# A four-layer graph kernel: attention sums that begin inside the decay layer, and zero counts moved into the first loop

## The chip, the cores and the metric

The kernel runs on one core of a Trainium2 chip. The metric is the device time of one execution in microseconds. A core has a matrix engine (PE, with its weight loads shown as PEld), a vector engine (DVE), a scalar engine (ACT), a general engine (POOL) and a queue engine (SP) that here issues nearly all DMAs. Each takes its instructions in order; semaphores tie them together.

## The reference

3327 nodes with 64 features `x` and a 0/1 matrix `adj` (3327 x 3327) go through four layers of the form `x = x + layer(relu(layernorm(x)))`:

- Layers 0 and 3 are hyperbolic attention: for each pair of nodes a sigmoid weight times `adj`, times a function (an arctangent) of the pair's inner products, then a weighted sum over neighbours.
- Layer 1 (the decay) weights a node's neighbours by their rank: `rank = cumsum(mask, axis=1)`, `w = mask * DECAY ** (k - pos)`, `out = w @ (h @ W) + bias`, with at most 100 neighbours.
- Layer 2 (the attention with gates) needs `(A > 0) @ h` with the diagonal of `adj` left out, an average of neighbours, and two GRU cells; their outputs are scaled by the diagonal of `adj` and added to `x`.

The kernel uses that `adj` holds only zeros and ones. It proves that on the fly: it counts the zeros and the ones of every block and compares the sum of the counts at the end; if they don't add up, a general path runs.

## The kernel before

The matrix is padded to 3328 = 26 blocks of 128 (`T` = 26), transposed, and read from memory block row by block row.

**First loop (layer 0, `hyperbolic_series`, lines 334 to 706).** Four chunks of columns (4, 3, 3 and 3 tiles of each half: 1024 or 768 columns) times 26 row blocks `b` make 104 tiles `k`. For each tile SP loads `adj` into one of four buffers (L386), ACT makes a sigmoid (L595), POOL multiplies it by `adj` (L597), PE makes the inner products (L608, L609), ACT takes the arctangent (L614), DVE combines both (L618), and PE sums over neighbours (L627, L635). An iteration `j` handles two tiles; the sigmoid and POOL's multiply are queued three tiles ahead, the load five. The order on ACT, DVE, PE and POOL is the one written in the program. Each iteration ends with `ahead.step(j)` (L1314): one DVE instruction for the next layer, alternately a mask (L1324) and a zero count (L1333) over half of a 128 x 1664 piece ("quarter") of `adj`, for the first twelve (`EARLY`) row blocks of layer 1, from four buffers of their own.

**Decay (layer 1, `plain_decay`, lines 1358 to 1604).** Two column halves `c` times 26 blocks make 52 steps `k`, in which `b` runs from 25 down to 0. `make_mask` turns a quarter of `adj` into an 8-bit mask, on POOL (L1413) or on DVE (L1410); `check` counts its zeros on DVE and issues the load that takes its buffer (L1399), of which there are seven. PE multiplies the mask by a triangular matrix to count ranks (`counts`, L1422), ACT turns counts into powers of two (`weights`, L1428), PE sums (`sums`, L1436). Twelve steps of counts run before `h` is normed; from then on each step catches up two sums until level, then does one. At the end of a half, `degrees` (L1443) copies the numbers of neighbours, `out_of` (L1451) the sums; `from_pairs` (L1256) multiplies by the layer's matrix and adds to `x`. Zero counts of the twelve quarters in `LATE` are left for layer 2.

**Attention and gates (layer 2, `plain_gat`, lines 1606 to 1803).** `norm_relu` norms all of `x`; then 26 blocks of 16 matmuls (L1708) multiply masks by two half-precision parts of `h`. Between blocks a table (`todo`) places other work: `turn` (transposes of `h`), `degrees`, `inverse`, and `check` for the `LATE` quarters, loaded a second time (L1630). Then eight GRU steps `u` (L1777): PE products (L1741, L1746), sigmoids, DVE before the tanh (L1759, L1760), tanh, and `state` on DVE (L1770 to L1774). The result is transposed back and added to `x` (L1266, L1801, L1802), outside the hand-ordered region, so that the scheduler slips it between the last states.

**Second loop (layer 3)** is the first loop's code with the 8-bit masks in place of `adj`.

Of the kernel before, what the change touches and what calls it, by code (L numbers as in the profile page):

```python
# [10 lines left out]
F32 = mybir.dt.float32  # L11
# [37 lines left out]
def tile_gnn4(ctx: ExitStack, tc: tile.TileContext, x, adjT, att0, b0, w1, bias1, w_gat, a_gat,  # L49
# [285 lines left out]
    def hyperbolic_series(r, params, ok, masks=None, done=None, ahead=None, then=None):  # L335
# [18 lines left out]
        with ExitStack() as st:  # L354
            pers = st.enter_context(room(name="hs", bufs=1))
# [235 lines left out]
            def sigmoid(k):  # L591
# [4 lines left out]
                adj = adjs.pop(k) if masks is None else halves(masks[b // 2][:, b % 2, :], c)  # L596
                G.tensor_tensor(sig, adj, sig, op=OP.mult)  # L597

# [207 lines left out]
            if then is not None:  # L806
                then(SimpleNamespace(Xr=Xr, M=M, slots=slots, later=later, factors=factors, close=lp.close,
                                     ahead=ahead))
                return
# [463 lines left out]
    LATE = *range(EARLY, EARLY + 4), *range(EARLY + 7, 2 * T - 4, 4)  # L1273
# [11 lines left out]
    class Ahead:  # L1285


        def __init__(self, masks, zo):
            self.masks, self.zo = masks, zo

        def begin(self, pool):
            self.adjs = [pool.tile([P, 2, CW], F32, name=f"ahead{k}") for k in range(4)]
# [20 lines left out]

        def step(self, j):  # L1314
# [3 lines left out]
            n = j - 2  # L1318
            q, i = divmod(n, 4)
            if 0 <= q < EARLY:  # L1320
                o, what = i // 2, i % 2
                adj = self.adjs[q % 4][:, o, :]
                if what == 0:
                    V.tensor_scalar(mask_of(self.masks, q)[:, o, :], adj, 1.0, 0.0, op0=OP.is_equal, op1=OP.add,  # L1324
                                    accum_out=self.ones, saturate=False)
                else:
                    k = q if o == 0 else 2 * T + 2 + q
                    zeros(self.same[:, o, :], adj, self.zo[:, k:k + 1])
            if n >= 3 and (n - 3) % 2 == 0 and (n - 3) // 4 < EARLY:
                self.load((n - 3) // 4 + 4, (n - 3) // 2 % 2)  # L1330
# [27 lines left out]
    def plain_decay(e, right, masks, zo, wt, bias, gru, ball_of_r):  # L1358
# [15 lines left out]
        with ExitStack() as st:  # L1374
# [12 lines left out]
            for k in (1, 0, 4, 3, 2):  # L1387
                w2 = masks[k].bitcast(BF)
                free += [w2[:, q, :].rearrange("p (o h i) -> p o h i", o=2, h=2) for q in range(2)]
            own = [pers.tile([P, 2, 2, BK], BF, name=f"w{i}") for i in range(3)]  # L1390
# [3 lines left out]
            def adj_of(k):  # L1394
                return bufs[(k - EARLY) % len(bufs)]
# [507 lines left out]
```

## Time and profile before

| | us |
|---|---|
| median of three runs (749.37 to 753.2) | 752.94 |
| the profiled execution | 750.64 |
| its span, first to last instruction | 748.8 |
| first loop, first to last sums | 34.3 to 242 |
| decay, first counts to last sums | 245.2 to 389.1 |
| attention's blocks | 408.7 to 450.4 |
| `x` of layer 2 ready | 486.6 |
| second loop, from its first sums | 516.9 to 720 |

| engine | busy us | share of the span |
|---|---|---|
| PE | 634.7 | 85% |
| ACT | 543.1 | 73% |
| DVE | 518.6 | 69% |
| POOL | 467.3 | 62% |

A profile line gives start and length, or busy time and count; `out<-in` names the tiles, and what follows a `<-` in brackets is what ended the engine's wait. "Issue" is time in which an engine waited for nothing that the profile shows. Ends of matmuls are modelled.

### The profile page before, as it was taken

The page shows a single profiled execution, that of the slowest core. Times are in us where ns is not written, and L with a number is a line of the kernel's source. Part 1 is how long each engine was busy: PE and PEld are TensorE (multiplying, and loading weights), DVE is VectorE, ACT ScalarE, POOL GpSimd, SP SyncE. Part 2 cuts the span into 40 slices and gives each one's busy share as a digit, 9 for nine tenths or more (in the row PEclk, how much of TensorE's full clock was granted, in tenths as well). Part 3 has the DMA queues.
Part 4 walks back from the last instruction along what each step waited for, and adds up shares of the span by engine and source line. Part 5 has one row for each costly group of instructions (what it writes and reads, how often), then busy time and mean ns, then how long its engine had stood idle before and what let it go on. Part 6 is the DMA issues. An engine that isn't in the chain of part 4 may idle for free.

```text
span 748.8 us, 11837 instructions
## 1 busy us (share of the span) xinstructions
PE 634.7 (85%) x4227; PEld 257.6 (34%) x4227; DVE 518.6 (69%) x909; ACT 543.1 (73%) x697; POOL 467.3 (62%) x353
## 2 busy tenths in 40 slices
PE   0799999999999788889982999328999999999950
PEld 0522233333333333434441663124223333333310
DVE  6867777777777698978828577996555555555556
ACT  2788888888887864577782369257888889889841
POOL 2699989989999002399910000036888788887830
PEclk9999999999999999999995999659999999999995
DMA  3988898988888600599813640001001001000001
GB/s 62 347 261 284 267 279 252 287 273 275 259 261 266 260 1 10 200 401 380 334 36 149 223 143 1 0 0 39 1 1 39 1 2 38 0 1 1 1 2 49
DMA packets 57028, 106.46 MB, mean 142 GB/s; under 512 B 8928, under 2 KB 33152, under 8 KB 56960
## 3 DMA queue, kind: packets, MB, share of 16 engines
q1 hardware_dynamic: 52608, 105.59, 42.5%
q10 hardware_dynamic: 4352, 0.02, 0.3%
q8 instruction: 35, 0.57, 0.3%
q14 instruction: 33, 0.27, 0.1%
HBM read 102.87 MB, written 0.88 MB: 139 GB/s over the span
## 4 chain that ended last, share of the span: by engine, by line
PE 59%; DVE 18%; ACT 8%; issue 7%; POOL 5%; DMA 1%; ACTq 1%; POOLq 0%; DVEq 0%
PE slot L627 16%; PE slot L635 9%; PE slot L608 8%; PE slot L1422 7%; PE slot L609 7%; PE bank L1708 5%; POOL sig L597 5%; PE slot L1436 4%; ACT sig L595 2%; DVE X L1473 2%; DMA adj<-in 1%; DVE mask L1410 1%; ACT slot L614 1%; ACTq L307 1%; ACT w L1428 1%
## 5 line engine op out<-in xcount | busy, mean ns | idle before, releaser
L618 DVE SCALAR_TENSOR_TENSOR sig<-slot,sig 128x768 f32<-128x768 f32 (+1 forms) x208 | 212.7, 1022 | 145.7 <-POOL sig L597 141.7
L614 ACT ACTIVATE slot<-slot 128x768 f32<-128x768 f32 (+1 forms) x208 | 177.3, 852 | 54.4 <-PE slot L609 54.2
L597 POOL TENSOR_TENSOR sig<-adj,sig 128x768 f32<-128x768 f32 (+1 forms) x104 | 201.0, 1962 | 14.2 <-ACT sig L595 10.0
L595 ACT ACTIVATE sig<-leftB,right 128x768 f32<-128x768 f32 (+1 forms) x208 | 203.2, 977 | 0.1
L597 POOL TENSOR_TENSOR sig<-mask,sig 128x768 f32<-128x768 fp8e4 (+1 forms) x104 | 173.2, 1677 | 40.4 <-ACT sig L595 35.0
L627 PE MATMUL slot<-sig,Xr 128*64 128x384 f32 (+1 forms) x832 | 169.6, 526 | 6.3 <-DVE sig L618 6.1
L608 PE MATMUL slot<-XC,XT 128*128 128x384 f16 (+1 forms) x416 | 142.2, 342 | 3.2 <-ACT sum L645 1.7
L609 PE MATMUL slot<-XF,XE 73*128 73x384 f16 (+1 forms) x416 | 141.4, 340 | 0.0
L635 PE MATMUL slot<-sig,X 128*32 128x384 f32 (+1 forms) x832 | 94.2, 525 | 0.0
L1428 ACT ACTIVATE w<-slot,ebias 128x832 bf16<-128x832 f32 x76 | 68.6, 951 | 30.7 <-PE slot L1422 30.6
L627 PEld LDWEIGHTS slot<-sig,Xr 128*64 128x64 f32 x832 | 49.6, 135 | 88.0 <-issue 61.5
L608 PEld LDWEIGHTS <-XT 128*128 128x128 f16 x416 | 40.6, 98 | 93.8 <-issue 67.4
L1422 PE MATMUL slot<-mask,rest 128*128 128x416 fp8e4 x208 | 55.0, 347 | 8.3 <-ACT mask L1428 4.2
L1413 POOL CAST mask<-ahead 128x1664 fp8e4<-128x1664 f32 x17 | 27.8, 1642 | 49.5 <-PE slot L1436 45.1
L1422 PE MATMUL slot<-mask,after 128*128 128x416 fp8e4 x208 | 54.7, 346 | 4.4 <-ACT deg L1443 2.9
L418 POOL MEMSET X<- 128x832 f32 x2 | 1.6, 791 | 84.4 <-ACT xh L1732 84.4
L1333 DVE TENSOR_SCALAR_CACHE_REDUCE same<-ahead 128x832 bf16<-128x832 f32 (+1 forms) x39 | 52.4, 1345 | 0.3
L609 PEld LDWEIGHTS <-XE 73*128 73x128 f16 x416 | 40.8, 98 | 29.7 <-issue 5.6
L1333 DVE TENSOR_SCALAR_CACHE_REDUCE same<-adj 128x1664 bf16<-128x1664 f32 x25 | 47.1, 1882 | 0.6
L1708 PE MATMUL bank<-mask,h 128*64 128x416 fp8e4 x416 | 40.1, 353 | 0.0
L635 PEld LDWEIGHTS slot<-sig,X 128*32 128x32 f32 x832 | 16.4, 108 | 67.7 <-issue 66.1
L1428 ACT ACTIVATE mask<-slot,ebias 128x832 bf16<-128x832 f32 x28 | 26.1, 952 | 11.5 <-PE slot L1422 11.3
(315 smaller groups left out, 636.6 us busy)
## 6 DMA issues: line engine op xcount, KB each, us to landing
adj<-in SPq DMA_DIRECT2D x78, 384.0 KB, 4.5
adj<-in SPq DMA_DIRECT2D x28, 832.0 KB, 6.8
ahead<-in SPq DMA_DIRECT2D x20, 832.0 KB, 8.3
adj<-in SPq DMA_DIRECT2D x27, 512.0 KB, 4.9
ahead<-in SPq DMA_DIRECT2D x32, 416.0 KB, 5.2
leftB<-left SPq DMA_DIRECT2D x6, 384.0 KB, 3.4
XC<-XT SPq DMA_DIRECT2D x12, 96.0 KB, 5.5
X<-in SPq DMA_DIRECT2D x2, 416.0 KB
```

The costliest lines, as they stand in the source:

```text
L595: A.activation(sig, leftB[c], AF.Sigmoid, bias=right[:, b:b + 1])
L597: G.tensor_tensor(sig, adj, sig, op=OP.mult)
L608: PE.matmul(L[:, o, :c[1] * P], XT[:, rows], XC[c][:, o, :], start=True, stop=False)
L609: PE.matmul(L[:, o, :c[1] * P], XE[:KE, rows], XF[c][:, o, :], start=False, stop=True)
L614: A.activation(L, L, AF.Arctan, scale=PA / SX ** 2)
L618: V.scalar_tensor_tensor(sig, slot[:, :, :tiles[k][0][1] * P], PC, sig, op0=OP.add, op1=OP.mult)
L627: PE.matmul(acc[c][o * D:(o + 1) * D, 0, :n], Xr[:, b, :], sigs[k][:, o, :], start=b == 0, stop=b == T - 1)
L635: PE.matmul(acc[c][q:q + 32, 1, :n], X0[:, b - 1 + i, :], w[:, o, :], start=b == 1, stop=b == T - 1, tile_position=(0, q))
L1333: V.tensor_scalar(same, adj, 0.0, 0.0, op0=OP.is_equal, op1=OP.add, accum_out=count)
L1422: PE.matmul(cnt[o][:, h, :BK], w, cols(k, o, h), start=w is after and steps[k][1] == T - 1, stop=True, skip_group_check=True)
L1428: A.activation(ws[k][:, o, :, :], cnt[o][:, :, :BK], AF.Exp, scale=-LN2, bias=ebias)
L1708: PE.matmul(acc[k][o * D:(o + 1) * D, :], w, mask[:, o * HP + k * BK:o * HP + (k + 1) * BK], start=b == T - 1 and i == 0, stop=b == 0 and ...
```

## The change

1. Six row blocks (`CHECKED`: b = 2, 6, 10, 11, 12, 13) have their zeros counted in the first loop, from the tile that the loop has loaded anyway: 24 counts, put on a list when the tile's POOL multiply is queued and run on DVE in the same iteration's `step`. The 48 masks and counts for the next layer are no longer one an iteration: a credit of 1.5 an iteration pays for both kinds. Their loads go out one iteration after the count.
2. `LATE` is gone, with the twelve loads and counts of layer 2. In the decay, steps of a `CHECKED` block have their mask made on DVE and no count. They are now 38 to 41, 45 and 49 in the second half, where they had been 27, 31, ... 47.
3. Catch-up steps no longer begin with two sums: one stands behind the first exponential, one behind the second. The first step of the second half and the end have an order of their own. All `degrees` but the first go to DVE.
4. Two of the four buffers of layer 1 become a pool of their own (`own`). From step 28 they take no more loads; `normed_h` writes the normed `h` of 12 of the 26 blocks there, one instruction (or pair) a step from step 33 on. Inverse roots are by `Ln` and `Exp`, whose table set is loaded at step 24.
5. `plain_gat` is called from within `plain_decay`, with its PSUM banks, inside the hand-ordered region. Blocks 0, 1 and 2 stand between the last products of the decay; then the other 14 blocks are normed (`finish`), while blocks of the first norm go on. The table `todo` and the order of blocks change; a weight product moves from ahead of the blocks to behind block 21.
6. The diagonals on POOL are made at every second step from 25 to 49 rather than at each step from 25 to 37.
7. The last transposes and updates of `x` move into the GRU loop (`last`), in program order.

```diff
@@ first loop
-                adj = adjs.pop(k) if masks is None else halves(masks[b // 2][:, b % 2, :], c)
+                adj = adjs[k] if masks is None else halves(masks[b // 2][:, b % 2, :], c)
                 G.tensor_tensor(sig, adj, sig, op=OP.mult)
+                if masks is None:
+                    ahead.see(k, b, adjs.pop(k))
...
-    LATE = *range(EARLY, EARLY + 4), *range(EARLY + 7, 2 * T - 4, 4)
+    CHECKED = 2, 6, 10, 11, 12, 13
...
+        def see(self, k, b, adj):
+            if b in CHECKED:
+                c = k // T
+                n = c * T + T - 1 - b if c < 2 else 2 * T + 2 + EARLY + (c - 2) * len(CHECKED) + CHECKED.index(b)
+                self.seen.append(lambda: zeros(self.same[:, :, :adj.shape[-1]], adj, self.zo[:, n:n + 1]))
...
+            for q, o in self.old:
+                self.load(q, o)
+            self.old, self.loads = self.loads, []
+            if j >= 2:
+                self.credit += 1.5
+                while self.seen:
+                    self.seen.pop(0)()
+                    self.credit -= 1
+                while self.credit >= 1:
+                    next(self.ops, None)
+                    self.credit -= 1
+            else:
+                while self.seen:
+                    self.seen.pop(0)()
@@ decay
-                if k not in LATE:
-                    zeros(same, adj_of(k), zo[:, k:k + 1])
-                load(k + len(bufs))
+                if steps[k][1] not in CHECKED:
+                    zeros(same, adjs[k], zo[:, k:k + 1])
+                buf = adjs.pop(k)
+                if k < T or not any(buf is t for t in ah_.own):
+                    load(next(coming), buf)
...
+                if c == 0 and o == 0:
+                    A.activation(to, cnt[o][q, :, :BK], AF.Copy, accum_out=total)
+                else:
+                    V.tensor_scalar(to, cnt[o][q, :, :BK], 1.0, 0.0, op0=OP.mult, op1=OP.add, accum_out=total)
...
+            norm0 = normed_h(slice(0, T // 4), M[:, :12, :], Xr[:, :12, :])
...
+                if k == T:
+                    counts(k - 1, 1, rest)
+                    degrees(0, 1)
+                    sum_next()
+                    for o in range(2):
+                        counts(k, o, after)
+                        weights(k, o)
+                    out_of(0)
                 elif k == K_:
                     counts(k - 1, 1, rest)
-                    degrees(steps[k - 1][0], 1)
+                    degrees(1, 1)
+                    sum_next()
+                    out_of(1)
+                else:
+                    counts(k, 0, after)
+                    weights(k, 0)
+                    if done < k - 1:
+                        sum_next()
+                    counts(k - 1, 1, rest)
+                    counts(k, 1, after)
+                    weights(k, 1)
+                    sum_next()
...
+                if k == T - 2:
+                    A.preload_act_table_set("natural_log_exp_and_others")
+                if k > T + 6:
+                    next(norm0, None)
...
+            then(H, hparts, banks, last_x, finish, close)
@@ attention
+            block(0)
+            last_x(0)
+            block(1)
+            last_x(1)
+            block(2)
+            finish()
+            close()
...
-                norm_relu(tp, hn, H.rearrange("p k o d -> p o k d"), order=(1, 0),
-                          then=lambda o: split2(*[p[:, :, o, :] for p in parts], H[:, :, o, :]))
...
+                todo = {5: lambda: turn(0), 10: lambda: degrees(0, 1), 12: lambda: degrees(2, 3),
+                        13: inverse, 15: lambda: turn(4), 17: lambda: turn(8), 19: lambda: turn(12),
+                        21: weights2}
+                for n in range(3, T):
+                    block(n)
+                    if n in todo:
+                        todo[n]()
...
+                def last(i):
+                    from_pairs(None, oP, use, None, range(4 * i, min(4 * i + 4, C2)),
+                               banks[4 + i].rearrange("p (t h d) -> p t h d", h=2, d=D))
...
+                    for i in {C + 2: (0,), C + 3: (1,), C + 4: (2, 3)}.get(u, ()):
+                        last(i)
```

The new `normed_h` norms the blocks `ks` of both halves in steps (each `yield` ends one):

```python
V.reduce_sum(s, x, axis=AX.X)
...
V.tensor_sub(mid, x, wide4(s))
...
A.activation(squares, mid, AF.Square)
...
V.reduce_sum(v, squares, axis=AX.X)
...
A.activation(y, v, AF.Ln)
A.activation(y, y, AF.Exp, scale=-0.5)
...
for o in range(2):
    V.scalar_tensor_tensor(to[:, o], mid[:, o], 0.0, y[:, o, :, None].to_broadcast([P, n, D]),
                           op0=OP.max, op1=OP.mult)
    A.activation(hi[:, o], to[:, o], AF.Copy, scale=SH)
...
for o in range(2):
    V.scalar_tensor_tensor(lo[:, o], to[:, o], SH, hi[:, o], op0=OP.mult, op1=OP.subtract)
```

## The prediction

> **What bounds the kernel now.** I read the page first, then busy time by stage, the groups, the timeline inside the first loop, and the chain of waits around the stage borders.
>
> ```profile
> span 748.8 us, 11837 instructions
> ...
> DVE  6867777777777698978828577996555555555556
> ```
>
> Two pair loops (slices 2 to 13 and 28 to 39) fill most of the span; between them stand the decay and the attention. DVE is at 70% through the first loop, 50% through the second. By stage (PE, PEld, DVE, ACT, POOL busy; granted clock; DMA share):
>
> ```profile
> 93.00:140.00 47.00, 46.33 (x304) 17.31 (x300) 36.11 (x54) 40.88 (x54) 43.96 (x25) 1.00 0.87 270
> ...
> 388.00:409.00 21.00, 5.17 (x31) 3.09 (x31) 12.97 (x21) 8.48 (x15) 0.00 (x0) 0.61 0.45 163
> 409.00:452.00 43.00, 42.92 (x442) 26.37 (x440) 29.85 (x34) 20.84 (x33) 0.00 (x0) 0.95 0.50 160
> ```
>
> The first loop is held by PE (46.3 of 47.0 us), with POOL at 94% and DMA at 87%: three resources nearly full, DVE at 77%. From 388 to 409 us PE works 5.2 of 21.0 us. This hole is what the change aims at. Then the attention's blocks are pure PE. The chain of waits shows the hole's end, and that its first four blocks (64 matmuls) run at 2.0 us each, against 2.81 us for two later:
>
> ```profile
> 394.65 1.96 DVE ln_s L144 x2
> ...
> 407.80 0.90 PE bank L1648 x2
> 408.70 8.02 PE bank L1708 x64
> ```
>
> In the first loop every weight product on DVE (L618) starts within 0.06 us of the end of POOL's multiply (L597), or directly behind a count. The timeline round tile 54 (chunk 2, b = 2), by SP, DVE and POOL:
>
> ```profile
> 138.38 2.33 SPq L386 DMA_DIRECT2D adj<-in  x2
> ...
> 142.83 1.01 DVE L1333 TENSOR_SCALAR_CACHE_REDUCE same<-ahead 128x832 bf16<-128x832 f32 x1
> ...
> 143.76 0.95 DVE L618 SCALAR_TENSOR_TENSOR sig<-slot,sig 128x768 f32<-128x768 f32 x1
> ...
> 145.87 1.82 POOL L597 TENSOR_TENSOR sig<-adj,sig 128x768 f32<-128x768 f32 x1 [0.35 <-DMA adj<-in]
> ```
>
> Tile 54's load is the second of the first line (issued about 140.2, when POOL has finished tile 50, whose buffer it takes); it lands at 145.8, just as POOL wants it. The ahead count of this iteration runs at 142.83. A count of tile 54 would stand there too, and wait 3 us.
>
> **What the skill says.** (1) The Trainium skill, "TensorE: Matmul & The Clock Gate", section "What's actually happening": PE runs at half clock after an idle window of about 3.4 us and at full clock once busy as long. The trace agrees: 0.61 in the hole, the slow first blocks after it. (2) "Perfetto Trace Analysis", section "Tensor Engine Instruction": ACT, DVE and GPSIMD are strict FIFO. So a DVE count that waits for a load holds the next L618; in the trace L618 at 143.76 stands behind the count of 142.83. (3) "DMA: Bandwidth & Descriptors", section "Anatomy of one DMA": 2.0 us plus bytes/436e9, told of another path; an estimate of 2.9 us for 384 KB. The trace has 4.5 us (median of the x78), and I use that. (4) "GPSIMD Engine Reference", section "1. Specifications": POOL shares its SBUF interface with VectorE and loses to two-port modes or two SBUF inputs. The counts read one tensor and take 0.94 us start to start for 832 elements, so no such mode; L597 keeps 1.807 us minimum, 1.826 median. I add nothing for POOL.
>
> **The change part by part.**
>
> *Zero counts in the first loop.* 24 counts are added: 6 of 1024 elements and 18 of 768. From 0.94 us for 832 (and 0.88 for an L618 of 768) I take 1.14 and 0.88: 22.7 us of DVE. DVE idles 52 us between 35 and 233 us (146.1 busy of 198), so the work itself fits; its place costs. (a) Iterations now hold 1 or 2 counts or masks, 1.5 on average, where they held 1. In steady state (tiles 43 to 47) L618 of an odd tile starts at 127.33; then 0.88 + 2 x 0.94 puts the next L618 at 130.09, its end at 131.05, while PE wants the slot for its product at 130.84: 0.2 to 0.3 us late. Every other such iteration passes it on, about 12 x 0.26 = 3 us; I take 2, since some merge with (b). (b) A count is issued at the end of the iteration in which POOL's multiply was queued, behind the iteration's second L618. For an even tile that is 2.9 to 3.0 us before POOL's start, for an odd one 0.9. Loads land 1 to 3 us ahead of POOL in this trace. Lined up tile by tile (load issue when POOL ends tile m-4, plus 4.6 us, or 6.2 in the first chunk), waits are: chunk 0, b 6, 10, 12: 2.9, 2.7, 3.1; chunk 1, b 2, 6, 10, 12: 1.3, 1.9, 0.3, 0.8; chunk 2: 2.1 to 3.0, 2.1, 0.3, 1.3; chunk 3: 1.8, 1.7, 0.6, 1.1; odd tiles about 0. The next L618 has 0.8 us to spare. Waits beyond 0.8 sum to 13 us; the 0.94 us of work that a count displaces, and POOL's own 3 us lag at the loop's start, take part back: I take 7. Sum: **+9** (from +3, all but (a) hidden, to +16, nothing taken back). The next load into a counted tile's buffer also waits for the count, but that ends before POOL's multiply does. With this count gone the stall would move nowhere else: POOL follows ACT, ACT follows PE.
>
> *Catch-up sums split.* A catch-up step takes 3.6 us (304.39, 308.11, 311.71) with ACT's exponentials exposed; split, PE alone needs about 3.0. But POOL's mask of step 24 waits for its load until 315.17, that of 25 runs 318.29 to 319.86, and PE starts step 25 at 320.03. These loads are released by DVE's checks from 305.25 on, which don't change: gain 0 to 0.2. I take **0**.
>
> *Half border.* Both degree copies stand on ACT between exponentials:
>
> ```profile
> 322.56 0.86 ACT L1443 ACTIVATE deg<-slot 64x832 f32<-64x832 f32 x1
> ...
> 325.17 0.86 ACT L1443 ACTIVATE deg<-slot 64x832 f32<-64x832 f32 x1
> ```
>
> With the second on DVE (behind a check, free at about 323.3) and the sums between, the next step's `rest` counts come at about 328.0 rather than 329.9: **-1.9** (0 to -3).
>
> *Norm of 12 blocks inside the second half.* DVE: 3 x 0.95, 4 x 0.54 and five small ones, 5.9 us over 14 steps of 2.34; DVE works 29.0 of 43.0 us there. ACT gets one 0.85 square, two 0.5 copies, two small; it idles 0.54 a step. Hidden. The table load (1.28 us in the trace) comes at step 24, where PE waits for masks anyway. Two of seven adjacency buffers retire: five loads in rotation at 2.34 us a step is 11.7 us a cycle against about 6.8 to 8.3 to land and 1.9 to check: fits, but less cover. If not, rival 3.
>
> *The hole.* The old span from the sums' end (389.1) to the blocks' end (450.4) is 61.3 us. New, back to back at full clock: wait for the last degrees on DVE 0.6; 26 blocks x 1.40 (22 warm ones took 30.9) = 36.4; the X products that move between blocks 1.17 + 0.85; turns and diagonals 2.7; weights (0.9 + 0.2) and waits for ACT copies 2.0: 43.7. The second norm (14 blocks, about 9.2 us of DVE and ACT from last X) hides behind blocks 2 to 11 (14 us). **-17.6** (-15 to -19). The 12 late checks (1.93 us each) and their loads vanish; DVE was not the bound there: 0.
>
> *Last rows inside the GRU loop.* Now in program order, each `last` sits ahead of the next PE products:
>
> ```profile
> 472.94 0.52 PE L1266 MATMUL pt<-ident,H 128*128 128x128 f32 x3 [1.16 <-ACT gate L1753]
> 476.29 0.90 PE L1266 MATMUL pt<-ident,H 128*128 128x128 f32 x3 [2.83 <-DVE H L1774]
> ```
>
> Products of step 7 (2.55 us) wait for state 5 (476.2) and one transpose; the tanh input comes at 479.2 instead of 476.15, 1.2 us of it covered by the row updates. Then 0.6 and 0.9 us for transposes at `last(1)` and `last(2)`: **+2.7** (0 to +4.5).
>
> Sum: 9 + 0 - 1.9 + 0 - 17.6 + 2.7 = **-7.8 us**. The profiled execution took 750.6 us with a span of 748.8; it becomes 741.0 and 742.8. The runs' median, 752.94, is 2.3 above that execution: **745**.
>
> **Rivals.** (1) *DVE's slack takes the counts in*: POOL and DMA run further ahead than I allow; loop +3, sum -14, **739**. For it: 52 us of DVE idle. Against: the load of tile 54 landed only as POOL began. (2) *Slower*: the counts' waits reach PE whole. The place is the DVE queue behind the second L618; the price is 24 us (the waits listed, undiminished), sum +7, **760**. It decides from a loop cost of 16.8 us. For it: PE, POOL and DMA are all near full, nothing can be made up. Against: 0.8 us of spare at each L618. (3) *The gap moves into the second half*: five buffers and DVE steps that wait for ACT starve the masks; 0.4 us a step over 20 steps, +8, **753**. Against: masks stand 6 us (step 30) to 9.6 us (step 51) ahead of PE.
>
> **Chances.** Forecast 0.50, rival 1 0.20, rival 2 0.16, rival 3 0.14. About 0.5% (3.8 us) is what tells apart from no change. Of the forecast (own range 740 to 750) a tenth lies within it. Faster 0.63, same 0.18, slower 0.19. Range 737 to 757: it leaves out the far end of rival 2 and little of rival 1.
>
> **What would show it.** The blocks begin within 1.5 us of the decay's last sums, clock 1.0 throughout; the first loop ends about 9 us later, with new DVE waits on `adj` loads, longest near b 2 and 6; steps 33 to 46 keep 2.34 us; PE stands idle ahead of the eighth GRU products. Wrong, if the loop grows by under 4 or over 15 us, or the second half's steps lengthen.

## The result and the profile after

The changed kernel takes 773.78 us (median of four runs, 771.01 to 777.49) against 752.89 for the kernel before: a ratio of 1.0292, with a 95% interval from 1.0239 to 1.0345. It is slower by 21 us, where 745 was forecast. The profiled execution took 773.8 us, 23.2 more than that of before.

The page after, span, DVE's and the DMA's rows of the 40 slices:

```profile
span 772.1 us, 11825 instructions
...
DVE  6768879778788678887684316797555555555555
...
DMA  3877887978978910297960000001001001000001
```

The late loads of layer 2 are gone: the DMA row is empty behind the decay. DVE's idle slices (4, 3, 1, at 405 to 463 us) now stand among the attention's blocks, where the kernel before had the late counts. By stage, with the same columns as before (PE, PEld, DVE, ACT, POOL busy; granted clock; DMA share; GB/s): part of the first loop, the decay's last steps, and the stretch from the last sums to the blocks' end:

```profile
100.70:152.30 51.60, 49.56 (x320) 18.51 (x320) 43.20 (x68) 43.12 (x57) 46.48 (x27) 1.00 0.85 258
399.00:414.90 15.90, 15.90 (x108) 7.04 (x108) 10.41 (x13) 10.79 (x12) 8.79 (x14) 0.99 0.16 56
414.90:465.70 50.80, 45.18 (x456) 28.65 (x454) 15.97 (x26) 20.74 (x36) 0.00 (x0) 0.97 0.01 1
```

The hole before the attention is filled: PE works 45.2 of 50.8 us at a granted clock of 0.97. The chain of waits at the place where the hole was (start, length, what):

```profile
413.73 0.41 DVE deg L1477
...
414.79 1.05 DVE deg L1477 x2
...
415.88 1.25 PE slot L1738 x12
```

Blocks begin directly behind the decay's last sums, with one wait for the last degrees. So the change does what it says, and it still loses. Stage by stage, in the two profiled executions (the blocks of the kernel before end at 450.9 us; 450.4, given above, is too early by half a microsecond):

| stage | before | after | difference | predicted |
|---|---|---|---|---|
| start to the end of the first weight product | 34.2 | 40.2 | +6.0 | 0 |
| first loop, to the last weight product | 207.9 | 219.2 | +11.3 | +9 |
| decay, first counts to last sums | 143.9 | 152.4 | +8.5 | -1.9 |
| last sums to the blocks' end | 61.7 | 50.8 | -10.9 | -17.6 |
| blocks' end to the first mean of layer 3 | 35.8 | 42.6 | +6.8 | +2.7 |
| second loop | 206.0 | 206.0 | 0 | 0 |

The differences sum to +21.7. The rest of the spans' 23.3 lies behind the last engine instruction, where no stage changed.

**The start.** DVE's timeline in the prologue after:

```profile
20.29 1.02 DVE L467 SCALAR_TENSOR_TENSOR Xp<-Xr,Xp 128x832 f16<-128x832 f32 x1
25.19 1.22 DVE L1360 TENSOR_SCALAR_CACHE_REDUCE same<-adj 128x1024 bf16<-128x1024 f32 x1 [3.88 <-DMA adj<-in]
...
26.34 1.02 DVE L467 SCALAR_TENSOR_TENSOR Xp<-Xr,Xp 128x832 f16<-128x832 f32 x1
```

The first of the new counts (tile 2) stands between the two halves of one prologue step, and waits 3.9 us for its load. It was written behind the prologue, in iteration -1, but needs nothing except its load, and the scheduler orders the prologue: the count was carried up. The first weight product comes 6 us late.

**The first loop.** The groups of the page (count, busy and mean ns, then idle time before and what ended most of it) show who waits now:

```profile
L598 POOL TENSOR_TENSOR sig<-adj,sig 128x768 f32<-128x768 f32 (+1 forms) x104 | 201.8, 1962 | 31.5 <-ACT sig L596 27.4
...
L611 PE MATMUL slot<-XC,XT 128*128 128x384 f16 (+1 forms) x416 | 142.5, 342 | 11.6 <-DVE sig L621 9.6
...
L1360 DVE TENSOR_SCALAR_CACHE_REDUCE same<-adj 128x768 bf16<-128x768 f32 (+2 forms) x40 | 54.5, 1362 | 18.0 <-DMA adj<-in 17.6
```

DVE's counts wait 17.6 us for `adj` loads: 3.9 us is tile 2's wait in the prologue, 2.0 us falls in the decay, and 11.7 us in the loop (from the list of waits between 35 and 260 us: total, how often, longest):

```profile
DVE same L1360 <- DMA adj<-in: 11.7, 9, 3.1
```

PE waits 9.6 us for DVE's weight products. One such place on DVE, and on POOL the multiplies around it:

```profile
155.47 0.95 DVE L1360 TENSOR_SCALAR_CACHE_REDUCE same<-adj 128x768 bf16<-128x768 f32 x1 [3.12 <-DMA adj<-in]
...
156.34 1.01 DVE L1327 TENSOR_SCALAR_CACHE_REDUCE mask<-own 128x832 fp8e4<-128x832 f32 x1
...
157.28 1.82 DVE L621 SCALAR_TENSOR_TENSOR sig<-slot,sig 128x768 f32<-128x768 f32 x2
```
```profile
153.50 1.82 POOL L598 TENSOR_TENSOR sig<-adj,sig 128x768 f32<-128x768 f32 x1 [0.24 <-DMA adj<-in]
155.51 1.81 POOL L598 TENSOR_TENSOR sig<-adj,sig 128x768 f32<-128x768 f32 x1 [0.20 <-DMA adj<-in]
```

The count and POOL's multiply at 155.51 wait for the same load. The weight product of the tile that POOL finished at 155.32 stands behind that count and a mask: it starts at 157.28, 2 us late. This is the strict order of DVE's queue that the prediction drew from the Trainium skill ("Perfetto Trace Analysis", section "Tensor Engine Instruction"), and the trace agrees.

**The decay.** Most steps of the second half take 2.34 us as before, but 43, 44 and 45 take 5.50, 5.04 and 4.03: 14.6 instead of 7.0. DVE, SP and POOL there:

```profile
387.03 1.03 DVE L1437 TENSOR_SCALAR mask<-adj 128x1664 fp8e4<-128x1664 f32 x1 [4.09 <-DMA adj<-in]
387.97 1.88 DVE L1360 TENSOR_SCALAR_CACHE_REDUCE same<-ahead 128x1664 bf16<-128x1664 f32 x1
```
```profile
377.13 6.11 SPq L1425 DMA_DIRECT2D adj<-in  x3
389.93 2.81 SPq L1425 DMA_DIRECT2D ahead<-in  x2
```
```profile
380.77 1.57 POOL L1440 CAST mask<-adj 128x1664 fp8e4<-128x1664 f32 x1 [10.68 <-DMA adj<-in]
...
388.74 1.57 POOL L1440 CAST mask<-ahead 128x1664 fp8e4<-128x1664 f32 x1
```

Two things meet. POOL has waited 10.7 us for the load of step 42's mask and is late from there: its mask of step 44 (388.74) ends when PE already waits for it. And DVE's mask of step 45 waits 4.1 us for its load; the count behind it, which would release a buffer, waits with it, so that SP issues no load between 383.2 and 389.9. DVE's steps of the norm stand in that queue too, and pass the delay on to ACT. The waits from 383 to 402 us:

```profile
ACT own L1585 <- POOL mask L1440: 6.4, 1, 6.4
...
PE slot L1451 <- POOL mask L1440: 3.0, 1, 3.0
PE slot L1451 <- ACT w L1457: 2.6, 1, 2.6
```

PE's first wait makes step 43 long. The second makes step 44 long: ACT's exponential stands behind a copy of the normed `h` (L1585), which starts at 393.63, when DVE has written its input (the first of two L1583 ends at 393.55; POOL's mask, which the list names, was done by 393.1). Step 45 is long because PE then runs at a granted clock of 0.58.

**Blocks and tail.** Between the blocks PE waits for DVE's use of a diagonal, and longest for a copy on ACT:

```profile
434.95 0.37 PE L1785 MATMUL slot<-diag,ones_bf 128*64 128x416 bf16 x2 [0.68 <-DVE deg L1792]
...
450.60 1.11 PE L1774 MATMUL slot<-ident,own 128*128 128x128 f32 x4 [3.51 <-ACT xh L1779]
451.64 4.09 PE L1738 MATMUL slot<-mask,own 128*64 128x416 fp8e4 x32
```

The two blocks behind that wait take 4.09 us where two others take 3.00. In the kernel before, four matmuls of two diagonals ran without a wait between them:

```profile
420.07 0.52 PE L1669 MATMUL bank<-diag,ones_bf 128*64 128x416 bf16 x4
```

And in the tail the eighth GRU products stand behind a transpose that waits for a state:

```profile
489.07 0.87 PE L1269 MATMUL slot<-ident,own 128*128 128x128 f32 x3 [3.58 <-DVE own L1875]
...
492.43 0.47 PE L1269 MATMUL slot<-ident,own 128*128 128x128 f32 x1 [2.48 <-DVE own L1875]
...
492.83 3.04 PE L1842 MATMUL slot<-xh,gw 128*64 128x416 f32 x8
```

The products themselves then take 3.04 us where seven others took 1.62 to 2.15. The granted clock is 0.50 from 488.0 to 497.6 us: PE comes back from idling at half clock, as the Trainium skill's "TensorE: Matmul & The Clock Gate", section "What's actually happening", says.

### The profile page after: what moved, and what is told of

It is laid out like the page before. It is cut to its first block, busy times and chain, and to the rows that moved or that the text cites. A ratio compares the mean times of both kernels' runs of the same rounds, so it can differ in the third digit from the quotient of the medians.

```text
span 772.1 us, 11825 instructions
## 1 busy us (share of the span) xinstructions
PE 646.0 (84%) x4227; PEld 259.5 (34%) x4227; DVE 522.3 (68%) x946; ACT 538.1 (70%) x693; POOL 465.0 (60%) x353
## 4 chain that ended last, share of the span: by engine, by line
PE 39%; DVE 16%; issue 15%; POOL 13%; DMA 7%; ACT 7%; ACTq 1%; POOLq 0%; SPq 0%; DVEq 0%
PE slot L630 11%; POOL sig L598 8%; PE slot L638 6%; DMA adj<-in 6%; PE slot L611 6%; PE slot L612 5%; PE slot L1738 3%; POOL mask L1440 3%; PE slot L1451 3%; ACT sig L596 2%; DVE X L1506 1%; PE slot L1842 1%; PE slot L1465 1%; DVE same L1360 1%; DVE sig L621 1%
## 5 line engine op out<-in xcount | busy, mean ns | idle before, releaser
L598 POOL TENSOR_TENSOR sig<-adj,sig 128x768 f32<-128x768 f32 (+1 forms) x104 | 201.8, 1962 | 31.5 <-ACT sig L596 27.4
L1360 DVE TENSOR_SCALAR_CACHE_REDUCE same<-adj 128x768 bf16<-128x768 f32 (+2 forms) x40 | 54.5, 1362 | 18.0 <-DMA adj<-in 17.6
L1738 PE MATMUL slot<-mask,own 128*64 128x416 fp8e4 x416 | 39.8, 346 | 0.4 <-DVE deg L1477 0.4
L1440 POOL CAST mask<-ahead 128x1664 fp8e4<-128x1664 f32 x8 | 12.6, 1570 | 44.0 <-PE slot L1465 44.0
L1457 ACT ACTIVATE mask<-slot,ebias 128x832 bf16<-128x832 f32 x28 | 25.7, 951 | 16.3 <-PE slot L1451 15.6
L1465 PE MATMUL slot<-w,h 128*64 128x416 bf16 x304 | 36.1, 362 | 0.0
```

The source lines that it names most:

```text
L1360: V.tensor_scalar(same, adj, 0.0, 0.0, op0=OP.is_equal, op1=OP.add, accum_out=count)
L1457: A.activation(ws[k][:, o, :, :], cnt[o][:, :, :BK], AF.Exp, scale=-LN2, bias=ebias)
L1738: PE.matmul(acc[k][o * D:(o + 1) * D, :], w, mask[:, o * HP + k * BK:o * HP + (k + 1) * BK], start=n == 0 and i == 0, stop=n == T - 1 and ...
```

## The experiments

Each run changes the changed kernel unless it says otherwise. Times are medians, ratios are to the kernel before on the same chip. The changed kernel's own ratio is 1.0292, so a ratio of 1.0219 means 0.73 points, some 5.5 us, won back. By these ratios no repair tried alone is clear of the changed kernel, whose interval begins at 1.0239; the runs with six buffers in the first loop and those with all repairs are. What each does is read from its own stage. Stage times come from the traces, one execution each, and have a spread of their own: among runs whose code for a stage is that of the changed kernel the loop took 217.2 to 220.6 us, the decay 148.8 to 153.0, last sums to blocks' end 50.6 to 52.2, the tail (blocks' end to the first mean of layer 3) 42.1 to 42.9.

### The first loop

**Tile 2's count in iteration 0.**

```diff
-            else:
+            elif j >= 0:
                 while self.seen:
                     self.seen.pop(0)()
```

> Only the first of the added zero counts (tile 2) moves: it is issued in iteration 0, behind the first weight products, and no longer before them. Theory A (that count was carried up into the prologue, where VectorE waits for its load): the first weight product ends near 34.3 us as in the kernel before, not at 40.2, and the time falls by 5 to 6 us, to 768. Rival (the prologue's loss is made up later anyway, because loads and GpSimd set the loop's pace): under 2 us, 772 or more.

Measured: 767.9 us, ratio 1.0219 [1.0187, 1.0252]. The first weight product ends at 34.25 us, as before. The loop behind it grew to 221.8 us, so that its last weight product comes 3.4 us earlier than in the changed kernel (256.0 against 259.4). The cause of the 6 us is shown; 2.6 of them show up again in the loop, where the counts now wait 14.9 us for loads.

**No counts in the first loop.** This kernel leaves out the search for zeros in the six row blocks, and the final comparison of the totals is made never true.

```diff
-            if b in CHECKED:
+            if False:
...
-                self.credit += 1.5
+                self.credit += 1.0
...
```

> Leaves out the 24 zero counts of the first loop altogether (the six row blocks are not searched for zeros; the final comparison of the totals is made never true), with the old pace of one ahead step an iteration. Theory A (the counts cost 6 us in the prologue and 11 in the loop): first loop 208 us from the first weight product to the last, time 756 to 757. Rival (the loop grew because the ahead loads are now issued one iteration later): loop still 215 us or more, time 763 or more.

Measured: 756.8 us, ratio 1.0084 [1.0065, 1.0103]; loop 206.8 us, last weight product at 242.55 (242.13 before). By ratio that is 15.6 us, by the last weight product 16.8: prologue and loop together fall back to the old time, so the loss up to there comes from the counts and the pace set for them, none from the ahead loads, which still go out an iteration later.

**Six buffers for the loop's adjacency tiles**, with tile 2's count in iteration 0 (not shown again).

```diff
-                adjs[k] = px.tile([P, 2, W], F32, name="adj", bufs=4)[:, :, :c[1] * P]
+                adjs[k] = px.tile([P, 2, W], F32, name="adj", bufs=6)[:, :, :c[1] * P]
```

> As the run with tile 2's count in iteration 0, and six instead of four buffers for the adjacency tiles of the first loop, so that a load can land before its count is due. Theory A-b (most of the loop's 11 us are waits of VectorE's counts for their loads): loop 211 to 213 us, VectorE's waits for adj loads under 5 us, time 760 to 763. Rival A-a (the place and number of the counts on VectorE cost the time, the loads don't): loop 217 us or more, time 767 or more. Rival A-c (DMA itself is full, and more buffers don't make loads earlier): the same 217 or more, with VectorE's waits for loads unchanged.

Measured: 758.75 us, ratio 1.0115 [1.0077, 1.0153]; loop 209.3 us. The groups of this run:

```profile
L598 POOL TENSOR_TENSOR sig<-adj,sig 128x768 f32<-128x768 f32 (+1 forms) x104 | 201.7, 1964 | 14.9 <-ACT sig L596 12.7
...
L611 PE MATMUL slot<-XC,XT 128*128 128x384 f16 (+1 forms) x416 | 142.1, 342 | 4.4 <-DVE sig L621 2.0
...
L1360 DVE TENSOR_SCALAR_CACHE_REDUCE same<-adj 128x768 bf16<-128x768 f32 (+2 forms) x40 | 54.4, 1359 | 2.7 <-DMA adj<-in 2.3
```

All 24 counts are still there and DVE is as busy with them (54.4 us), but their waits for loads fall from 17.6 to 2.3 us, none of it in the loop (the 2.3 us is one wait in the decay); PE's for DVE fall from 9.6 to 2.0, POOL's for ACT from 27.4 to 12.7. The loop is 1.4 us longer than before, instead of 11.3. Against the run with tile 2's count in iteration 0 alone, which differs only in the buffers, its last weight product comes 12.4 us earlier (243.55 against 256.0). DMA was not full: it brought the tiles earlier as soon as it had somewhere to put them.

**Each count one iteration later**, with six buffers and tile 2's count in iteration 0.

```diff
...
-                while self.seen:
-                    self.seen.pop(0)()
+                while self.due:
+                    self.due.pop(0)()
                     self.credit -= 1
+                self.due, self.seen = self.seen, []
```

> As the run with six buffers, and each count issued one iteration later, after GpSimd has used the same tile, so that it never waits for a load. Theory A-b: loop 209 to 212 us, time 758 to 762. Rival A-a (number and place): loop 215 us or more, time 765 or more.

Measured: 758.84 us, ratio 1.0105 [1.0074, 1.0136]; loop 209.4 us. No better than the six buffers alone. Up to the last weight product the 24 counts cost 17.3 us: 3.4 for tile 2's place in the prologue, 12.4 for waits for loads, 1.4 for their number and place on DVE.

### The decay

**One more buffer in rotation.**

```diff
-            bufs = [*ah_.adjs, *[pers.tile([P, 2, CW], F32, name=f"adj{i}") for i in range(3)]]
+            bufs = [*ah_.adjs, *[pers.tile([P, 2, CW], F32, name=f"adj{i}") for i in range(4)]]
```

> One more adjacency buffer in the decay, so that six stay in rotation when two retire. Theory B (five buffers are too few: steps 43 to 45 take 14.6 us where three steps of 2.34 us make 7.0, because a load waits for a buffer that a queued check would release): steps 43 to 45 together 7 to 9 us, decay from the first counts to the last sums 145 to 147 us instead of 152.4, time 766 to 768. Rival (the loss comes from the norm's steps on VectorE and ScalarE, whatever the buffers): steps 43 to 45 stay at 13 us or more, time 772 or more.

Measured: 768.25 us, ratio 1.0226 [1.0187, 1.0264]; steps 43 to 45 take 2.34, 3.56 and 2.47 us, 8.4 together; decay 143.8 us, less than expected. What step 44 still loses is one wait:

```profile
PE slot L1451 <- ACT w L1457: 1.2, 1, 1.2
```

This exponential too stands behind the norm's copy on ACT, so the rival has a part, of 1.2 us. Seven buffers in rotation, as the kernel before has, weren't tried, nor five without the norm's steps.

**The check ahead of the mask.**

```diff
-                if EARLY + 7 <= k + LEAD < K_:
-                    make_mask(k + LEAD)
                 if LAG + 5 <= k < K_ - 1:
                     check(k + 1)
+                if EARLY + 7 <= k + LEAD < K_:
+                    make_mask(k + LEAD)
```

> In the decay's steps the check of step k+1, which releases a buffer, is issued ahead of the mask of step k+3 and not behind it; five buffers stay in rotation. Theory B (the mask of step 45 stands in VectorE's queue waiting for its load, and holds the checks that would release buffers): most of the 7.6 us of steps 43 to 45 comes back, at least 4, and the decay takes 145 to 149 us, time 767 to 770. If the number of buffers alone matters, under 2 us comes back, time 772 or more.

Measured: 766.95 us, ratio 1.0211 [1.017, 1.0252]; steps 43 to 45 take 5.18, 2.34 and 2.35, 9.9 together; decay 146.3 us. DVE's timeline of this run round the same mask:

```profile
379.15 1.89 DVE L1360 TENSOR_SCALAR_CACHE_REDUCE same<-ahead 128x1664 bf16<-128x1664 f32 x1
...
383.28 1.03 DVE L1437 TENSOR_SCALAR mask<-adj 128x1664 fp8e4<-128x1664 f32 x1 [2.23 <-DMA adj<-in]
```

The mask still waits, but a check that stood behind such a mask has gone out ahead of it, and steps 44 and 45 lose nothing. Step 43 still loses 2.8 us to POOL's late mask. Both readings of theory B hold: too few buffers, and a queue in which the release stands behind the wait. Of the 7.6 us the buffer takes 6.2, the order 4.7.

### Blocks and tail

**Turn and diagonal banks from different tiles.** PSUM's eight banks come as four tiles of two. A weight product's bank moves as well, from the sixth to the seventh.

```diff
...
-                    pt = bank(4 + t0 // 4 % 2)
+                    pt = bank((4, 6)[t0 // 4 % 2])
...
-                    dg = bank(6 + k % 2)[:, :BK]
+                    dg = bank((6, 5)[k % 2])[:, :BK]
```

> The transposes of the attention and the diagonal sums take turns on PSUM banks of different tiles (fifth and seventh bank, sixth and seventh) and no longer on two banks of one tile. Theory C (two banks of one tile are held as one, so transposes wait for ScalarE's copies from the other bank): the wait of 3.5 us before the transposes of blocks 8 to 11 goes, the stretch from the last sums to the blocks' end is 45 to 48 us instead of 50.8, time 769 to 771. Rival (ScalarE's inverse makes the copies late in any case): the stretch stays at 50 us or more.

Measured: 767.34 us, ratio 1.0199 [1.0153, 1.0245]; last sums to blocks' end 45.3 us instead of 50.8. PE's timeline of this run:

```profile
443.89 0.66 PE L1774 MATMUL slot<-ident,own 128*128 128x128 f32 x4
...
447.80 0.33 PE L1774 MATMUL slot<-ident,own 128*128 128x128 f32 x1 [0.32 <-ACT xh L1779]
```

The transposes of blocks 8 to 11 (443.89) go straight through, and so do the diagonals. ACT's inverse still stands ahead of the copies; it just doesn't matter when the next transposes write to another tile. The Trainium skill ("PSUM — Partial Sum Buffer", section "PSUM bank collisions raise a hardware error") reports that accesses to different banks run clean, and asks for a guard by bank and quadrant. The waits here are coarser than that: they follow the tile of two banks. In the kernel before, where each bank is a tile of its own, and in this run the waits between banks are gone.

**The rows behind the GRU loop.**

```diff
-                    for i in {C + 2: (0,), C + 3: (1,), C + 4: (2, 3)}.get(u, ()):
-                        last(i)
+                for i in range(4):
+                    last(i)
```

> The four calls that turn the attention's result back to rows stand behind the loop of GRU products again. Theory D (inside the loop their transposes wait for VectorE's state at the head of TensorE's queue and hold the eighth products): blocks' end to the first mean of layer 3 is 36 to 39 us instead of 42.6, time 768 to 771. Rival (the tail is longer because of what VectorE has to do): it stays at 41 us or more, time 772 or more.

Measured: 767.31 us, ratio 1.0196 [1.0148, 1.0244]; tail 37.7 us instead of 42.6. The eighth products in this run:

```profile
484.89 1.62 PE L1842 MATMUL slot<-xh,gw 128*64 128x416 f32 x8
...
486.44 0.93 PE L1847 MATMUL slot<-xh,gw 64*64 64x416 f32 x8
```

They follow the seventh without a wait and at a granted clock of 1.00. Of the 6.8 us, 4.9 are explained. Of the other 1.9, 1.3 lie at the start of the GRU loop: the third step's products start 7.7 us behind the blocks' end, where they started at 6.4 in the kernel before. One suspect there: ACT's copies of an accumulator now wait 0.66 us for DVE's read of the neighbour bank, where four ran through before. The changed kernel, then the kernel before:

```profile
467.08 1.03 ACT L1827 ACTIVATE xh<-slot 64x416 f32<-64x416 f32 x2 [0.66 <-DVE deg L1828]
```
```profile
450.38 2.13 ACT L1726 ACTIVATE xh<-bank 64x416 f32<-64x416 f32 x4 [7.47 <-PE bank L1708]
```

**All banks in another order**, so that neighbours lie in different tiles.

```diff
-            banks = [t[:, i, :] for t in (cnt[0], cnt[1], acc[0], acc[1]) for i in range(2)]
+            banks = [t[:, i, :] for ts in ((cnt[0], cnt[1]), (acc[0], acc[1])) for i in range(2) for t in ts]
```

> Only the order of the eight banks changes: neighbours in the list (accumulators 0 and 1, 2 and 3, the two turn banks, the two diagonal banks) now lie in different two-bank tiles. Theory C, carried on (reads of two banks of one tile are put in order even where nothing is written): last sums to blocks' end 45 to 46 us instead of 50.8 as in the run with the turn banks alone, and the start of the GRU loop shortens too, ScalarE's first copies run without the 0.66 us gaps for VectorE: tail 41 to 41.8 us instead of 42.6. Rival (the gaps at the start of the GRU loop come from VectorE's and ScalarE's own work): tail 42.4 us or more.

Measured: 770.64 us, ratio 1.0225 [1.0192, 1.0258]; last sums to blocks' end 45.4 us, as expected, but the tail grew to 46.9. ACT at the start of the GRU loop of this run:

```profile
459.96 2.11 ACT L1827 ACTIVATE xh<-slot 64x416 f32<-64x416 f32 x4 [5.25 <-PE slot L1738]
...
463.60 1.10 ACT L1854 ACTIVATE gate<-slot,gs 128x416 f32<-128x416 f32 x2 [1.53 <-PE slot L1847]
```

The gaps between the copies are gone (four in a row), but the sigmoids of gate r now wait for the last products of a step (L1847), which write gate h in the other bank of r's tile. It fits the same rule of the tiles, at another place. PE then waits 2.8 us for DVE and runs the next products at a granted clock of 0.62.

**Only the accumulators in another order.**

```diff
-            acc = [bank(k)[:, :BK] for k in range(C)]
+            acc = [bank(k)[:, :BK] for k in (0, 2, 1, 3)]
```

> Only the four accumulators of the attention are dealt differently to the first four banks (first, third, second, fourth), so that those read one after the other lie in different two-bank tiles; the GRU's gates keep their banks. Theory C, carried on: ScalarE's copies at the start of the GRU loop run without the 0.66 us gaps, and the tail is 40.8 to 41.8 us instead of 42.6. Rival: the gaps go, but VectorE's row work sets the loop's end: tail 42.3 us or more.

Measured: 773.14 us, ratio 1.027 [1.0234, 1.0305]; tail 42.3 us. PE in this run:

```profile
472.39 1.62 PE L1842 MATMUL slot<-xh,gw 128*64 128x416 f32 x8 [1.88 <-DVE deg L1828]
```

The gaps are gone and the tail isn't shorter: in this order as in the changed kernel's the products of the second step wait (1.9 and 2.0 us) for DVE's reads of the accumulators, whose tiles they take, and the third step starts 7.7 us behind the blocks' end in both. Taking the gaps away doesn't shorten the loop; another wait stands in their place.

### Together

**The repairs together**: tile 2's count in iteration 0, six buffers in the loop, six in rotation and the check first, separate turn banks, rows behind the GRU loop.

> The five repairs together: tile 2's count in iteration 0, six adjacency buffers in the first loop, six in rotation in the decay and the check ahead of the mask, turns on banks of different tiles, the rows behind the GRU loop. If the theories A to D hold side by side, their savings add: 759 as measured with the first two, less 8.6 in the decay, 5.5 in the blocks and 4.9 in the tail: 740 (737 to 744), which is faster than the kernel before by 1.1 to 1.9%. If a saving is only passed on to a later wait, 746 or more.

Measured: 741.44 us, ratio 0.9857 [0.9827, 0.9886]: 32 us under the changed kernel and 1.4% faster than the kernel before. Loop 209.2 us, decay 144.6, last sums to blocks' end 45.3, tail 38.8. The repairs add up, but for 1 us of the tail, where one GRU step runs at a granted clock of 0.57. Span, PE's and DVE's row:

```profile
span 740.7 us, 11834 instructions
...
PE   0899999999999796999999989149999999999940
...
DVE  6878888888887598888985319995554555555555
```

**The rows one iteration later, inside the GRU loop**, with the other repairs.

```diff
-                    for i in {C + 2: (0,), C + 3: (1,), C + 4: (2, 3)}.get(u, ()):
+                    for i in {C + 3: (0,), C + 4: (1,), C + 5: (2, 3)}.get(u, ()):
```

> As the run with the five repairs, but the rows are turned back inside the GRU loop, one iteration later than in the changed kernel, when no products are left to issue. Theory D (only products behind a waiting transpose lose): the tail is 34.5 to 37 us instead of 37.7, time 1 to 3 us under that run. Rival (VectorE's row updates between the states cost as much as they hide): tail 37.5 us or more, time the same or higher.

Measured: 740.71 us, ratio 0.9855 [0.9828, 0.9882]; tail 37.9 us. The rival holds: moving the rows into the loop brings nothing over leaving them behind it, even when no products stand behind them.

**The counts among the blocks again**, with the other repairs: none in the first loop, whose pace goes back to one step an iteration, and twelve loads and counts between the attention's blocks.

```diff
-            if b in CHECKED:
+            if False:
...
+                late = [k for k in range(EARLY, 2 * T) if T - 1 - k % T in CHECKED]
...
+                    if n in (6, 8, 9, 11, 12, 14) or n > 16:
+                        check()
...
```

> As the run with the five repairs, but the zero counts of the six row blocks stand among the attention's blocks, on late loads, as in the kernel before, and not in the first loop. If moving the counts is worth nothing once it is hidden (theory A: both places have slack), first loop 208 us instead of 209, last sums to blocks' end 45 to 47 us, time within 3 us of that run. If the late checks hold VectorE or ScalarE there, the stretch is 49 us or more and the time 4 us or more higher: then moving the counts was a gain of its own.

Measured: 743.21 us, ratio 0.9903 [0.9873, 0.9934]. The loop takes 207.8 us (1.4 less), last sums to blocks' end 48.3 (3.0 more), the tail 40.9 (2.1 more). The decay took 142.8, but with the same code for it the runs of this section range from 142.2 to 146.0. The result lies between the two expectations: the median is 1.8 us higher than with the counts in the loop, and the intervals of the two just overlap. Whether moving the counts is a gain of its own, once it is hidden, isn't settled; by these stages it is a few microseconds at most.

**The norm behind the second half**, with the other repairs.

```diff
-                if k > T + 6:
-                    next(norm0, None)
```

> As the run with the five repairs, but no step of the first 12 blocks' norm is issued inside the decay's second half: all follow behind its last step. Theory (the norm is hidden there, and outside it stands in the way of the first block): last sums to blocks' end 52 to 56 us instead of 45.3, decay 143 to 145 us, time 747 to 751. Rival (the norm's steps cost the second half as much as they save): decay 3 us or more shorter than in that run.

Measured: 750.17 us, ratio 0.9985 [0.9972, 0.9997]. Last sums to blocks' end 54.6 us instead of 45.3, decay 144.9. Steps 43 to 45 take 7.0 us here and 7.8 with the norm among them, so the norm costs 0.8 us inside the second half and saves 9.3: most of the 10.8 us by which the repaired kernel is faster than the kernel before.

**The last two bank orders with the other repairs**: all banks reordered, and the accumulators alone.

> The five repairs with this bank order in place of the separate turn banks. Theory C, carried on: last sums to blocks' end 45 to 46 us, tail 36 to 37 us as in the kernel before (35.8) and not 37.7 to 38.8, time 739 to 741. Rival: tail 37.7 us or more, time 741 to 743.

> The five repairs with this order of the accumulators. Theory C, carried on: tail 36 to 37 us (37.7 to 38.8 without it), time 739 to 741. Rival: tail unchanged.

Measured: 742.38 us (0.9879 [0.9856, 0.9903], tail 39.5) and 742.09 us (0.9859 [0.9833, 0.9886], tail 37.7). Neither brings the tail under the 37.7 to 38.8 us that it takes without them. Why the tail keeps its last 1.9 us stays open; that two-bank tiles make the second GRU products wait for both of their accumulators is argued from the two waits above, not shown.

## Why the prediction was wrong

From the forecast sum of -7.8 us to the measured +21.7 there are 29.5 us. They lie in the decay (10.4, of which 7.6 at steps 43 to 45), the hole (6.7), the start, for which the sum has no term (6.0), the last rows (4.1) and the first loop (2.3). The step that failed most is the norm inside the second half, put at nothing because five loads in rotation "fits". The prediction's own sign of being wrong, that the second half's steps lengthen, came about.

*Zero counts in the first loop, +9.* The loop grew by 11.3, within the stated +3 to +16, and the mechanism, counts that wait for loads and hold weight products, is what the runs show. That the number is close is in part luck: the prediction listed waits of some 24 us and let 7 of them reach PE, the rest being taken up by 0.8 us of spare at each weight product. The counts wait 11.7 us in the loop, half as long, and the loop loses nearly all of it (with tile 2's count in iteration 0, 12.4 for 14.9 us of waits). Number and place: 2 predicted, 1.4 measured. What failed besides is the start of the sum. It counted the loop from its first weight product and took every count to stay where it was written; its list of waits for chunk 0 begins at b = 6, and tile 2 (b = 2) is not in it. That count was not held by the hand-written order and moved into the prologue: +6.0. Up to the last weight product the counts cost 17.3 us, just over the 16.8 at which rival 2 was to decide. So rival 2's outcome came about, though only two thirds of it in the place that it named.

*Catch-up sums split, 0.* Nearly right: the lag behind the kernel before is 17.4 us at step 11 and again at step 22. The steps that don't wait fell from 3.6 to 3.27 us, and the ones that wait for masks gave it back. Step 22, which takes 3.27 us instead of 1.98, and the two behind it add 1.1.

*Half border, -1.9.* Right in kind: steps 25 and 26 take 6.48 us where they took 7.89, -1.4.

*Norm inside the second half, 0.* The norm itself is nearly hidden (0.8 us with six buffers). The sentence "Two of seven adjacency buffers retire: five loads in rotation ... fits, but less cover" failed. It compared the cycle of five buffers with an average of landing and checking. But the rotation is no average: a mask on DVE waits for a load, the release of the next buffer stands behind it in the same queue, and the load that would end the next wait isn't issued. Three steps lose 7.6 us. Rival 3 had the price (+8) and the buffers, but spread it over 20 steps and had DVE wait for ACT; here DVE waits for loads, and ACT for DVE. The margin quoted against it, masks 6 to 9.6 us ahead of PE, was that of a kernel with seven buffers, with DVE masks at other steps. Step 37 adds 0.6, where ACT's square of the norm waits 0.8 us for DVE; with six buffers that step takes 2.34 us again.

*The hole, -17.6.* It became -10.9. The estimate of 43.7 us for the new stretch assumed free banks and full clock. 5.5 us are waits for the other bank of a tile and the slower blocks behind the longest of them; without them the stretch is 45.3. More than half of the other 1.6 is the price of a block: 64 matmuls take 5.74 us up to the next instruction, 1.43 a block where 1.40 was taken, some 0.9 over 26 blocks. Blocks cost the same in the kernel before (from 435.20 to 450.95 us there are eleven); the estimate had let them end at 450.4. The prediction read the new code for which bank is used when, and didn't ask what the program treats as one buffer. In the kernel before each bank was a tile of its own; the change took over the two-bank tiles of the decay.

*Last rows in the GRU loop, +2.7.* Right in mechanism and sign. What was mis-sized is the price of the eighth products: 2.55 us in the sum, 4.6 measured, because PE came to them at half clock after waits of 3.58 and 2.48 us for states. With that the 2.7 come near the 4.9 us that moving the rows back returns. The other 1.9, of which 1.3 lie at the start of the GRU loop, had no term, and their cause is open.

The rivals were priced one at a time. Rivals 2 and 3 both came about, with two losses that no case held: the hoisted count and the banks. With all five repairs the change saves 10.8 us, more than the 7.8 forecast.

## What to carry to other kernels

- When work is moved into a queue, ask first what it waits for, not how long it runs: 24 counts on an engine with 52 us to spare cost 17 us, and 1.4 us with two more buffers and one count moved. An instruction with few dependencies can also rise above the code that it was written behind.
- A release that stands behind a wait in the same queue turns a short wait into a stall of the whole rotation; release first, and don't judge a rotation by its mean.
- Where buffers are handed from one stage to the next, look at how they were allotted: here waits followed the tile of two banks. Put things used alternately, by different engines, into different tiles.

## What the runs showed that was not expected

- Two more buffers of 4 KB a partition took the counts' waits in the first loop from 14.9 us to none, although the DMA share was 0.82 to 0.87 in that loop in all these runs.
- In PSUM tiles of two banks, even two reads (ACT's copy and DVE's product, 0.66 us) were put one behind the other, and a sigmoid waited 1.53 us for products written to the other bank. With the neighbours in different tiles the same copies ran without these waits.
- Short waits of PE came back as slow matmuls: behind one of 3.51 us two blocks took 4.09 us for 3.00, behind waits of 3.58 and 2.48 us the eighth products took 3.04 for 1.62. Such a loss belongs to the price of the wait.
